# Layer 0 of a four-layer network: new slots for the steps of a hand-written schedule, and a new order of the steps within a slot

## The chip, the cores and the metric

The kernel runs on one core of one Trainium2 chip. The metric is the device time of one execution in microseconds (us); for a kernel it is given as the median of several executions. The core's engines run side by side, each in its own program order: TensorE (PE; its weight loads are PEld), VectorE (DVE), ScalarE (ACT), GpSimd (POOL) and SyncE (SP), whose queue issues nearly all DMAs. They wait for each other by semaphores.

## What is computed

Four layers follow each other on `x` of shape (4, 96, 64, 64): layer 0, which is changed, and three that stay as they are (a 7x7 depthwise convolution with a feed-forward part; attention without softmax and a quantized feed-forward part; a Fourier mixing step and another quantized feed-forward part). Layer 0 holds two Mamba blocks over each image's 4096 tokens, then a 1x1 convolution together with a pooled term, a normalization over the batch, and a residual. Cut to what matters:

```python
def _mamba_block(seq, ...):                      # seq: (4, 4096, 96), DIN = 192, DSTATE = 16
    h = layernorm(seq) * ln_g + ln_b
    xs, z = jnp.split(h @ in_w, 2, axis=-1)
    xc = silu(causal_conv4(xs) + conv_b)
    dbl = xc @ xproj_w
    dt, Bm, Cm = dbl[..., :6], dbl[..., 6:22], dbl[..., 22:]
    delta = softplus(dt @ dt_w + dt_b)
    dA = exp(delta[..., None] * A)               # per channel and state
    dBx = delta[..., None] * Bm[:, :, None, :] * xc[..., None]
    hstates = scan over tokens: hs[t] = dA[t] * hs[t - 1] + dBx[t]
    y = einsum('blds,bls->bld', hstates, Cm) + Dp * xc
    return (y * silu(z)) @ out_w                 # added to seq
```

192 channels times 16 states make 3072 recurrences per image and block, each over 4096 tokens. The scan is the bulk of the work.

## The kernel before

**Items and scans.** `layer0` (from line 147) works on 32 items: 4 stretches of 1024 tokens, times 2 blocks, times 4 images, in that order (the list `items`). An item has 24 scans, each one DVE instruction over 128 partitions (32 channels by 4 states) and 1024 tokens (L643). A scan is named (p, g, j): p is one of three parts of the channels, j one of two halves of a part, g one of four groups of states. `SLOTS['order']` gives the order: scans 0 to 5 are (0,0,0), (0,0,1), (0,2,0), (0,1,0), (0,1,1), (0,2,1); 6 and 7 are (0,3,0), (0,3,1); 8 to 17 are those of p = 1 and, mixed among the last of them, (2,3,0) and (2,3,1); 18 to 23 are the rest of p = 2.

**Slots.** The order of the instructions on PE, DVE, ACT and POOL is written out by hand: the loop at the end of `layer0` runs over steps m; `divmod(m, 24)` is the item k and the slot t. In slot t of item k DVE gets scan t of item k, and the other entries of `SLOTS` say in which slot each other step is put into its engine's order. A slot is only a place in the order; an engine starts an instruction when its turn comes and its semaphores are there. `SLOTS['seq']` gives the order of the kinds of steps within one slot. SP's DMAs are not held to the slots: they stand in SP's queue in about the order in which the steps were recorded, and each waits for its data and buffer, with all behind it.

**The steps of a slot.**
- `scan` (L623 on): for g = 0 and 1 a DVE product (L636) of `udb` (delta times xc, spread over the states) with `rep`, then the scan (L643). At j = 0 it takes one of four `hs` buffers from a first-in, first-out list.
- `fill` (L587 on): PE makes `rep` in one of two PSUM tiles. For g = 0 and 1 it spreads a row of B (L599). For g = 3, called GA, it transposes `uta` eight times (L594); `uta` is delta times xc times B, made by ACT in 32 weighings (L507), the entry `weigh`. `fills` gives how many slots ahead of its scan each fill stands.
- `exp` (L610): ACT makes `da`, the decay of a scan, three slots ahead (one slot ahead into PSUM, `dap`, for g = 2, called GP). `da` has three buffers.
- `b` (L621): GpSimd's product `up` for the scans of GP, at slots `b`. `c` (L648): GpSimd multiplies both halves of a finished (p, g) by C (`crep`), one slot behind its last scan; c(p, g) below.
- `start` (L658): PE begins y of a part with Dp times xc, at `starts`; `sum` (L665): PE adds a (p, g) after its c, at `sums` (a row for each p, an entry for each g), and this frees the `hs` buffer; `gate` (L677): DVE multiplies y by silu(z), at `gates` (values over 23 fall in the next item).
- `keep` (L654): ACT copies the last column of a finished scan into `state`.
- `end`: the output, at slots `ox` (load of x), `px` and `pz` (PE, L684 and L301), `fin` (ACT and the store, L710).
- `stages`: the first stage of the next item, function `first_stage` (L333 on). A slot value v of these entries stands at slot floor(v) - 24 counted from that item's scan 0, so 14.2 is slot 14 of the item before it and 28 is slot 4 of its own. Steps of one slot stand in the order of v. They are: load of x (`ln_ld`), the normalization (`ln_*`), the convolution's three products (`xc`, L287, with ACT's copies L411), Silu of xc and of the item before's z together with two loads of ACT's tables (`silu`, L422, L528, L304), `xproj` (PE, L301) and ACT's two copies into `dbl` (L441), delta's three products and copies, Softplus (`soft`, L449), the transposes of B (`tb`) and their copy (`bt`, L463), the stores `dd` and `du` (after GpSimd's product L479), z's products, `turn` and `keep` of delta times xc (L488, L493), the weighings, and the loads from DRAM `load_d` (`ddb`), `load_u` (`udb`), `load_c` (`crep`) and `load_b` (`brep`), four or eight DMAs of 128 KB each.

The loop itself:

```python
for m in range(first, last + 19):
    k, t = divmod(m, NTL)
    for step in SLOTS["seq"]:
        steps[step](m, k, t)
```

After the last item the totals of the batch normalization follow, and then layer 1.

Of the kernel before, what the change touches and what calls it, by code (L numbers as in the profile page):

```python
# [44 lines left out]
for _name, _w in [("A", 48), ("Dp", 6), ("c_b1", 3), ("f2_b1", 3), ("f3_b1", 3), ("id", 48), ("rd", 48), ("rb", 48), ("ib", 48)]:  # L45
# [2 lines left out]
NV128 = _n  # L48


SLOTS = {'ln_ld': -22,
 'ln_c': -9.4,
 'ln_sq': -9.2,
 'ln_sc': -7,
 'ln_t': -6.8,
 'ln_ev': -6.4,
 'xc': ((-6, -2.4), (-3.8, 0.4), (-1.2, 2.2)),
 'silu': 2.2,
 'xproj': 4.6,
 'dbl': 4.6,  # L60
 'delta': ((5.2, 6), (6, 7.4), (7.4, 8)),
 'soft': 8.2,
 'tb': 7.4,
 'dd': 8.6,
 'bt': 12.8,
 'du': 11.6,
 'z': ((11.4, 11.4), (10.8, 11.6), (12.6, 12.6)),
 'turn': (14.2, 15, 16),
 'keep': (14.4, 15.8, 16),
 'weigh': ((18, 5), (19, 4), (20, 6), (21, 2), (22, 2), (24, 7), (25, 1), (26, 2), (28, 3)),  # L70
 'load_d': ((14.4, 21.6), (24.6, 28.4), (29, 35.8)),
 'load_u': (14, 26.4, 33.6),
 'load_c': (20.2, 22.2, 24.8, 27.8),
 'load_b': 20.2,
 'fills': {(0, 1, 0): 2,
           (0, 3, 0): 1,
           (0, 3, 1): 1,
           (1, 0, 0): 1,
           (1, 3, 0): 1,
           (1, 1, 0): 1,  # L80
           (1, 3, 1): 1,
           (2, 3, 0): 1,
           (2, 3, 1): 1,
           (2, 0, 0): 1,
           (2, 1, 0): 2,
           (0, 0, 0): 1},
 'sums': ((7, 9, 8, 11), (13, 18, 17, 20), (24, 26, 26, 23)),
 'starts': (5, 13, 18),
 'gates': (13, 26, 31),
 'b': (2, 5, 8, 17, 20, 22),  # L90
 'fill0': -9,
 'ox': 25,
 'px': 33,
 'pz': 33,
 'fin': 34,
 'state': 1,
 'seq': ('scan', 'fill', 'end', 'start', 'b', 'keep', 'gate', 'c', 'sum', 'exp', 'stages'),
 'order': [(0, 0, 0), (0, 0, 1), (0, 2, 0), (0, 1, 0), (0, 1, 1), (0, 2, 1), (0, 3, 0), (0, 3, 1), (1, 0, 0),
           (1, 0, 1), (1, 2, 0), (1, 3, 0), (1, 1, 0), (1, 1, 1), (1, 2, 1), (2, 3, 0), (1, 3, 1), (2, 3, 1),
           (2, 0, 0), (2, 0, 1), (2, 2, 0), (2, 1, 0), (2, 1, 1), (2, 2, 1)]}  # L100
# [2 lines left out]
class Net:  # L103
# [43 lines left out]
    def layer0(self, dram, scratch):  # L147
        tc, nc, ins = self.tc, self.nc, self.ins
        x_in = ins["x"]
        with ExitStack() as ctx:  # L150
# [65 lines left out]
            def until(slot):  # L216
                for m in sorted(m for m in stages[0] if m <= slot - 24):
                    for _, f in sorted(stages[0].pop(m), key=lambda x: x[0]):
                        f()

            def prepare():
                with tc.tile_pool(name="l0s", bufs=1) as wk, tc.tile_pool(name="l0g", bufs=1) as sums_pool:
# [14 lines left out]
                    def spread_taps(q):  # L237
                        at = slice(q * MB, (q + 1) * MB)
                        ps = wide(C + 1, MB, q)
                        nc.tensor.matmul(ps, one, row[:, at], start=True, stop=True)  # L240
                        nc.vector.tensor_copy(taps[:, at], ps)
# [19 lines left out]

                    until(SLOTS["xc"][1][1])
                    spread_taps(2)
# [69 lines left out]
            def first_stage(k):  # L333
# [5 lines left out]
                def at_slot(t):  # L339
                    def keep(f):  # L340
                        steps.setdefault(int(t // 1) - 24, []).append((t, f))

                    return keep

                @at_slot(SLOTS["ln_ld"])
                def _():
                    m["xn"] = load_x(b, s, i) if k else x0


                @at_slot(SLOTS["ln_c"])  # L350
                def _():
# [9 lines left out]

                @at_slot(SLOTS["ln_sq"])
                def _():
# [15 lines left out]

                @at_slot(SLOTS["ln_sc"])  # L380
                def _():
# [3 lines left out]

                @at_slot(SLOTS["ln_t"])
                def _():
# [1344 lines left out]
```

## Time and profile before

| what | value |
|---|---|
| times of three runs | 3705.59, 3710.8, 3724.08 us; median 3710.8 |
| the profiled execution | 3723.78 us, of which the span of the profile is 3722.0 us |
| layer 0, first start to last end of a scan | 73.67 to 2449.02 us |
| mean ns of one scan, of one product on DVE | about 2340, about 1215 |
| mean ns of one product c, of one product `up` on POOL | 4187, 2363 |
| mean ns of one `da`, of one weighing on ACT | 1146, 441 |
| DMA, share of 16 engines over the span | 46.2% in queue q1 |

A page of the profile holds the busy time of each engine (part 1), the span in 40 equal slices of about 93 us, where each digit is the busy share of a slice in tenths (part 2), the DMA queues, the chain that ended last, and the costliest groups of instructions. Beside the page the trace answers questions: the waits, where a row such as `DVE hs L643 <- PE rep L594: 41.5, 34, 3.2` says that DVE, ahead of its instruction of line 643, was idle for 41.5 us in total, 34 times, 3.2 at most, until PE's instruction of line 594 released it; and the timeline, whose rows begin with the start and the busy time in us, then engine, line, operation and tiles, how many instructions stand in the row, and in brackets the idle time ahead of them with what ended it. Busy times of instructions that follow each other on one engine overlap by up to 0.1 us, so that steps are counted from start to start.

### The profile page before, as it was taken

To read this page: it belongs to the slowest core of one execution; us is meant where nothing else is said; L and a number is where in the kernel's file an instruction comes from. 1 tells how busy PE (TensorE), PEld (TensorE's weight loads), DVE (VectorE), ACT (ScalarE), POOL (GpSimd) and SP (SyncE) were. 2 spreads that over 40 slices of the span, in tenths; PEclk is the share of its full clock that TensorE was granted. 3 is DMA by queue.
4 is the path that set the end of the run, shared out by engine and by line. 5 is a ranking of instruction groups with operands and counts; after the bars stand their busy time and mean duration, and the time that the engine had idled before them with its cause. 6 is when DMAs were issued, how large, how long until landed. Compare 5 with 4: busy or idle time off the path is not lost. (4 is left out here: it accounts for less than half of the span.)

```text
span 3722.0 us, 47365 instructions
## 1 busy us (share of the span) xinstructions
PE 3098.0 (83%) x15360; PEld 1409.3 (38%) x15360; DVE 3020.9 (81%) x2966; ACT 2722.6 (73%) x5584; POOL 2567.9 (69%) x925
## 2 busy tenths in 40 slices
PE   7888788878887888888888878659798888999888
PEld 3332223222322232223222322228345436667643
DVE  5999999999999999999999999962665693444649
ACT  5888888887888887888888878641346786656557
POOL 1989988899899988998998999832001263444427
PEclk8999999989999999899999999859899998999989
DMA  7666656665666666666666666557000000011001
GB/s 186 151 162 155 170 152 161 156 169 153 160 155 169 160 153 156 172 158 152 158 171 160 148 165 160 145 149 272 12 0 1 1 1 6 24 35 47 24 12 58
DMA packets 171552, 446.36 MB, mean 120 GB/s; under 512 B 48756, under 2 KB 50750, under 8 KB 167968
## 3 DMA queue, kind: packets, MB, share of 16 engines
q1 hardware_dynamic: 171304, 443.34, 46.2%
q8 instruction: 121, 1.98, 0.2%
q14 instruction: 127, 1.04, 0.1%
HBM read 369.68 MB, written 73.50 MB: 119 GB/s over the span
## 5 line engine op out<-in xcount | busy, mean ns | idle before, releaser
L648 POOL TENSOR_TENSOR hs<-hs,crep 128x2048 f32<-128x2048 f32 x384 | 1601.7, 4187 | 224.4 <-DVE hs L643 177.2
L610 ACT ACTIVATE da<-ddb,nega 128x1024 f32<-128x1024 f32 x576 | 660.1, 1146 | 200.3 <-DMA ddb<-dd 129.1
L643 DVE TENSOR_TENSOR_SCAN hs<-da,state,rep 128x1024 f32<-128x1024 f32 x288 | 669.5, 2338 | 47.8 <-PE rep L594 28.0
L621 POOL TENSOR_TENSOR up<-udb,brep 128x1024 f32<-128x1024 f32 x192 | 453.6, 2363 | 83.3 <-DMA udb<-ud 62.2
L665 PE MATMUL y<-hs,sel_r 128*32 128x512 f32 x3072 | 462.2, 696 | 12.2 <-POOL hs L648 11.9
L599 PE MATMUL rep<-dbl,sel_b 32*128 32x512 f32 x768 | 249.9, 729 | 215.6 <-DVE hs L643 215.5
L507 ACT ACTIVATE uta<-delta,bt 128x192 f32<-128x192 f32 x1024 | 379.7, 441 | 0.0
L287 PE MATMUL ps<-n,w_x 97*64 97x512 f32 x1536 | 354.5, 604 | 12.5 <-ACT xc L411 11.8
L643 DVE TENSOR_TENSOR_SCAN hs<-da,state,u 128x1024 f32<-128x1024 f32 x144 | 338.1, 2348 | 23.7 <-PE y L665 7.8
L643 DVE TENSOR_TENSOR_SCAN hs<-dap,state,up 128x1024 f32<-128x1024 f32 x144 | 335.3, 2328 | 1.5 <-ACT dap L610 1.4
L594 PE MATMUL rep<-ident,uta 128*128 128x128 f32 x1536 | 223.0, 287 | 103.6 <-DVE hs L643 89.9
L594 PEld LDWEIGHTS rep<-ident,uta 128*128 128x128 f32 x1536 | 175.2, 146 | 248.6 <-issue 136.2
L636 DVE TENSOR_TENSOR u<-udb,rep 128x1024 f32<-128x1024 f32 x192 | 235.3, 1226 | 25.0 <-DMA udb<-ud 11.4
L643 DVE TENSOR_TENSOR_SCAN hs<-da,rep 128x1024 f32<-128x1024 f32 x96 | 218.0, 2281 | 19.5 <-PE rep L594 13.5
L610 ACT ACTIVATE dap<-ddb,nega 128x1024 f32<-128x1024 f32 x192 | 214.1, 1115 | 24.8 <-DVE hs L643 24.3
L636 DVE TENSOR_TENSOR rep<-udb,rep 128x1024 f32<-128x1024 f32 x192 | 231.8, 1207 | 0.0
L1290 POOL CAST hq<-y 128x1536 fp8e5<-128x1536 f16 x64 | 94.0, 1469 | 198.2 <-DVE y L1289 136.3
L287 PEld LDWEIGHTS ps<-n,w_x 97*64 97x64 f32 x1536 | 105.1, 137 | 259.1 <-issue 208.8
L665 PEld LDWEIGHTS y<-hs,sel_r 128*32 128x32 f32 x3072 | 73.9, 119 | 337.1 <-issue 261.7
L599 PEld LDWEIGHTS rep<-dbl,sel_b 32*128 32x128 f32 x768 | 65.8, 205 | 353.5 <-issue 299.1
L658 PE MATMUL y<-xc,dp 128*128 128x512 f32 x192 | 132.0, 778 | 31.3 <-ACT bt L463 31.3
L1157 POOL MEMSET h<- 1x4096 f32 x1 | 3.5, 3507 | 215.0 <-ACT g L1039 215.0
(287 smaller groups left out, 6291.6 us busy)
## 6 DMA issues: line engine op xcount, KB each, us to landing
udb<-ud SPq DMA_DIRECT2D x768, 128.0 KB
ddb<-dd SPq DMA_DIRECT2D x768, 128.0 KB
crep<-cd SPq DMA_DIRECT2D x512, 128.0 KB
dd<-delta SPq DMA_DIRECT2D x64, 384.0 KB
band<-in_band SPq DMA_DIRECT2D x24, 1024.0 KB
ud<-delta SPq DMA_DIRECT2D x62, 384.0 KB
brep<-cd SPq DMA_DIRECT2D x128, 128.0 KB
x<-in_x SPq DMA_DIRECT2D x32, 384.0 KB
```

The costliest lines, as they stand in the source:

```text
L287: nc.tensor.matmul(ps[rows], w[:, 64 * p : 64 * p + 64], rhs[:, at.start + shift : at.stop + shift], start=k == 0, stop=k == len(ws) - 1, ...
L507: nc.scalar.mul(m["uta"][:, q, :, 32 * s4 : 32 * s4 + 32].rearrange("t (p j) d -> t p j d", p=3), m["udt"][:, :, q].rearrange("t p (j d) - ...
L594: nc.tensor.transpose(x[:, q * 128 : q * 128 + 128], made[k]["uta"][:, q, 2 * h + j], self.ident)
L599: nc.tensor.matmul(x[:, at], sel_b[rows, g], made[k]["dbl"][rows, at], start=True, stop=True)
L610: nc.scalar.activation(da, made[k]["dd", h, j], AF.Exp, scale=nega[:, col : col + 1])
L621: nc.gpsimd.tensor_mul(up, made[k]["ud", p][:, j], made[k]["brep", GP])
L636: nc.vector.tensor_mul(u, made[k]["ud", h][:, j], x)
L643: nc.vector.tensor_tensor_scan(hs[:, 1:], made[k].pop(("da", t)), u, st, ALU.mult, ALU.add)
L648: nc.gpsimd.tensor_mul(hs[:, :, :T], hs[:, :, 1:], twice(made[k]["crep", g]))
L658: nc.tensor.matmul(y, dp[:, items[k][2], p], made[k]["xc"][:, p], start=True, stop=True)
L665: nc.tensor.matmul(made[k]["y", p][row : row + 32], sel_r, made[k]["hs", p, g][:, j, at], start=False, stop=True, skip_group_check=True,)
L1290: nc.gpsimd.tensor_copy(q, y2, saturate=False)
```

## The change

Only values in `SLOTS` change; no function does, and each instruction of layer 0 is still issued once for each item. The core of the diff:

```diff
-SLOTS = {'ln_ld': -22,
+SLOTS = {'ln_ld': -20.4,
...
- 'xc': ((-6, -2.4), (-3.8, 0.4), (-1.2, 2.2)),
- 'silu': 2.2,
+ 'xc': ((-6, -3.6), (-3.8, 0.4), (-1.2, 1.8)),
+ 'silu': 3.6,
...
- 'delta': ((5.2, 6), (6, 7.4), (7.4, 8)),
- 'soft': 8.2,
+ 'delta': ((5.2, 6.6), (6, 6.6), (7.2, 8.4)),
+ 'soft': 8.4,
...
- 'dd': 8.6,
+ 'dd': 9.2,
- 'du': 11.6,
- 'z': ((11.4, 11.4), (10.8, 11.6), (12.6, 12.6)),
- 'turn': (14.2, 15, 16),
- 'keep': (14.4, 15.8, 16),
- 'weigh': ((18, 5), (19, 4), (20, 6), (21, 2), (22, 2), (24, 7), (25, 1), (26, 2), (28, 3)),
- 'load_d': ((14.4, 21.6), (24.6, 28.4), (29, 35.8)),
- 'load_u': (14, 26.4, 33.6),
- 'load_c': (20.2, 22.2, 24.8, 27.8),
- 'load_b': 20.2,
- 'fills': {(0, 1, 0): 2,
+ 'du': 12.4,
+ 'z': ((12.4, 12.6), (12, 12.6), (13.6, 13.6)),
+ 'turn': (14, 15.4, 16.4),
+ 'keep': (14.4, 15.8, 16.8),
+ 'weigh': ((18, 2), (19, 2), (20, 11), (21, 6), (23, 3), (24, 1), (26, 1), (27, 1), (28, 5)),
+ 'load_d': ((18.4, 18.4), (25.6, 26.4), (29.2, 35.6)),
+ 'load_u': (13, 22.8, 33),
+ 'load_c': (21, 20.2, 24.4, 24),
+ 'load_b': 19.2,
+ 'fills': {(0, 1, 0): 1,
...
-           (1, 1, 0): 1,
+           (1, 1, 0): 2,
...
-           (2, 1, 0): 2,
+           (2, 1, 0): 1,
...
- 'sums': ((7, 9, 8, 11), (13, 18, 17, 20), (24, 26, 26, 23)),
+ 'sums': ((7, 9, 9, 11), (13, 16, 17, 18), (23, 27, 26, 22)),
  'starts': (5, 13, 18),
- 'gates': (13, 26, 31),
- 'b': (2, 5, 8, 17, 20, 22),
- 'fill0': -9,
- 'ox': 25,
+ 'gates': (13, 25, 29),
+ 'b': (0, 4, 13, 14, 19, 21),
+ 'fill0': -11,
+ 'ox': 32,
...
- 'seq': ('scan', 'fill', 'end', 'start', 'b', 'keep', 'gate', 'c', 'sum', 'exp', 'stages'),
+ 'seq': ('scan', 'exp', 'start', 'b', 'fill', 'gate', 'c', 'sum', 'end', 'keep', 'stages'),
```

The four values of `load_c` are for g = 3, 0, 1, 2; the six of `b` are for (0,1), (1,0), (1,1), (2,0), (2,1) and (0,0) of the next item.

In the order within a slot this moves `exp` ahead of the state copies, of the output's copies and of the stages on ACT; `start` ahead of `fill`, and the output's products behind the sums, on PE. On DVE and POOL the order of the kinds within a slot stays.

## The prediction

> **What bounds the kernel now.** I read the page first: parts 1 and 2 say which engine is full, and when.
>
> ```profile
> PE 3098.0 (83%) x15360; PEld 1409.3 (38%) x15360; DVE 3020.9 (81%) x2966; ACT 2722.6 (73%) x5584; POOL 2567.9 (69%) x925
> ...
> DVE  5999999999999999999999999962665693444649
> ```
>
> The whole change lies in layer 0, and DVE is at 9 in every slice of layer 0 but the first. Its scans run from 73.67 us (first start) to 2449.02 us (last end): 32 items, mean 74.3 us from scan 0 to the next scan 0 (shortest 72.1, longest 77.4). So only DVE's idle time can be won, and the second view is what DVE waits for in that stretch:
>
> ```profile
> DVE hs L643 <- PE rep L594: 41.5, 34, 3.2
> DVE hs L643 <- PE y L665: 9.9, 32, 0.7
> ```
>
> The first row is nearly all one place: scan 7 of an item, (0,3,1), waits for fill(7), TensorE's eight transposes of `uta`. From the timeline, scan 6 to scan 7 takes 3.69 us on average over items 3 to 29 where other scans follow each other in 2.25: 1.44 us per item. Third view, the timeline of item 18 (scan 0 at 1409.88), where it is worst:
>
> ```profile
> 1427.09 1.13 ACT L507 ACTIVATE uta<-delta,bt 128x192 f32<-128x192 f32 x3
> 1428.13 1.04 ACT L441 COPY dbl<-ps 102x512 f32<-102x512 f32 x2
> ...
> 1428.54 1.92 PE L658 MATMUL y<-xc,dp 128*128 128x512 f32 x2
> ...
> 1430.38 1.98 PE L287 MATMUL ps<-dbl,dtw 103*64 103x512 f32 x4
> ...
> 1432.29 1.97 PE L594 MATMUL rep<-ident,uta 128*128 128x128 f32 x8
> ...
> 1434.37 2.35 DVE L643 TENSOR_TENSOR_SCAN hs<-da,state,rep 128x1024 f32<-128x1024 f32 x1 [3.23 <-PE rep L594]
> ```
>
> Behind fill(6) TensorE's queue holds the start of y (L658), then delta's first product (L287), which needs ACT's `dbl` copies, and only then fill(7). The same four steps in item 21 (TensorE alone):
>
> ```profile
> 1650.72 1.32 PE L594 MATMUL rep<-ident,uta 128*128 128x128 f32 x8 [1.73 <-DVE hs L643]
> 1651.88 1.02 PE L658 MATMUL y<-xc,dp 128*128 128x512 f32 x2
> 1652.83 1.08 PE L287 MATMUL ps<-dbl,dtw 103*64 103x512 f32 x4
> 1653.84 1.09 PE L594 MATMUL rep<-ident,uta 128*128 128x128 f32 x8
> ```
>
> Here each is half as long, and scan 7 hardly waits (0.06 us). Items fall into these two kinds: the start takes 1.5 to 1.9 us in 19 of items 1 to 30, about 1.02 in 11. ACT's own largest wait is the fourth view (300 to 2400 us):
>
> ```profile
> ACT da L610 <- DMA ddb<-dd: 117.1, 29, 5.5
> ```
>
> That is 4 us per item, before exp(1): its rows `ddb`(0,1) are issued on SP behind a `crep` load that waits for GpSimd. DVE has cover there, but ACT comes late to the next slots.
>
> **The change, part by part.** Times count from scan 0 of an item; "e5" is the end of scan 5.
>
> *Order within a slot, start and fill.* TensorE gets start(0) of slot 5 ahead of fill(6) instead of behind it. There it lies in TensorE's wait for e4 (idle 2.01 us in item 18, 1.73 in 21), so it costs nothing; if `xproj` ended over 1 us later it would delay fill(6). What fill(7) then waits for is the end of the `dbl` copies, plus 0.1, plus delta's product, plus its own time. Doing this for items 1 to 30 with each item's own durations, fill(7) ends **0.59 us** earlier on average (0.06 in items of the short kind, about 1.0 in the long).
>
> *ACT: exp leads, silu from 2.2 to 3.6, `weigh`, `load_d`.* `load_d`(0,1) goes from 21.6 to 18.4, ahead of the `brep` and `crep` loads: the 4 us wait goes. 24 instead of 19 of the 32 weighings come before slot 24: five at 0.345 = 1.7 us more there. ACT is so 2.3 us early at slot 0 and next waits for e0 (dap(2)'s bank) and e1 (the state copy of slot 2), e1 = 5.92. From there, with start-to-start times of item 17: state copy 0.10, weighing 0.35, exp(6) 1.05, weighing 0.35 (silu begins at about 7.8); table, silu, silu of z, table 5.45; dap(5) 1.04; exp(7) 1.04; five weighings 1.73; `dbl` 1.05: end at 18.1. Before it is 18.29 in item 17 and 18.35 on average. **0.25 us** earlier.
>
> *gate(2) from slot 7 to 5, gate(1) from 2 to 1.* DVE's work stays. gate(2) (0.6 us) leaves the stretch from scan 7 to 11, and this gives nothing: from the end of fill(7) to that of fill(11) TensorE runs without a break for 12.33 us (items 10, 12, 17, 20, 25), and scan 11 starts 0.05 us behind fill(11) in most of them. DVE would need 11.7 for its part now, so it waits the 0.6 at scan 11 instead. What counts is when fill(7) ends, both terms above.
>
> *GpSimd's products.* up(1,1) goes from slot 8 to 13, up(2,0) from 17 to 14: both now between du and c(1,1), where GpSimd idles 4.3 us, for 4.7 us. Worked through with item-by-item times, c(1,3) ends 1.9 us after scan 18 starts. The sum (1,3) moves to slot 18, ahead of xc's first product; TensorE reaches it 1.46 us after scan 18 now, so 0.4 us of waiting. fill(21) then ends at 7.6; DVE wants it at 8.2. Hidden by 0.65, and fill(0) of the next item by 0.5 (0.94 now less 0.4). The other sums, `up` slots, and fill leads have over 0.8 us each between ready and needed; an `hs` slot is free at least as early as now, so the 9.9 us of the second row may shrink: I take nothing.
>
> *SP's queue.* ddb(1,0) and (1,1) now stand behind `crep`2, which waits for c(2,2) (ends at 7.6 in item 18). Eight `crep` issues and four `ddb` at about 0.45: 13.3; landing about 3.5 later (item 18's ddb(0,1): last issue ends at 71.6, exp(1) starts at 75.1): 16.8. ACT comes to exp(8) at 18.1: hidden by 1.3. `x` for the output (`ox` 25 to 32) follows `cd`, at about 20.5; x0 took 4.6 us from issue to its first reader (1.7 to 6.3), TensorE wants it at 27: hidden by 2.
>
> *Ends.* At the start ACT does an `xc` copy (0.47 us) ahead of exp(0): +0.5. At the end the last two sums of y both wait for c(2,2) where now one is done before; one took 1.93 us there: **+2**, once.
>
> *Sum.* 31 x (0.59 + 0.25) = 26, less 2.5: 23.5 us. The profiled execution took 3723.8 us (span 3722.0), 13 above the median of 3710.8. 3700.3/3723.8 of the median is **3687**. Bounds: the first term from 0.06 to 1.0, the second from 0 (weighings eat ACT's lead) to 0.5: 31 x 0.06 - 2.5 = nothing, to 31 x 1.5 - 2.5 = 44.
>
> **The rivals.**
>
> 1. *TensorE stays in its short kind.* The start now fills part of the gap ahead of fill(6). If this makes all items like item 21 there, fill(7) ends 1.12 us earlier instead of 0.59: 31 x 1.37 - 2.5 = 40, **3671**. For: the rows of items 18 and 21, a factor of two. Against: the gaps change by under 1 us, and the 6.5 us gap before fill(3) stays. [...]
>
> 2. *The gain is met by a next wait.* fill(11), fill(21) and fill(0) all have under 1 us of cover, dap(23) about 0.4. If 0.5 of the 0.84 us comes back there: 31 x 0.34 - 2.5 = 8, **3703**. For: the shortest interval now, 72.1, shows how little is left. Against: these covers are worked out, and each wait shifts the next.
>
> 3. *Slower: TensorE queues behind GpSimd at sum (1,3).* If c(1,3) ends more than 0.65 us later than worked out (`brep` late, products slower than 2.36), xc's products, fill(21) and scan 21 move 1:1. At 2.5 us late: 31 x (2.5 - 0.65) = 57 against 26: **3744**. For: du, two products and three c's now run without a gap. Against: GpSimd catches up before c(1,0) in every item from 2 to 29 (c(1,0) starts 0.15 to 0.45 us after e9).
>
> That the change does nothing is no rival: the built order has start ahead of fill(6), and the loads moved, in every item.
>
> **How the numbers follow.** Forecast (3677 to 3698) 0.42; TensorE short (3655 to 3677) 0.20; met by a next wait (3698 to 3724) 0.27; slower (above 3724) 0.11. Likeliest: 3687. The range 3655 to 3724 leaves out the slower case. About 0.5% (18.6 us) is what a measurement of this kernel tells from no change. Faster by more than that is below 3692: all of the second case and four fifths of the first, 0.54. Slower by more is above 3729: 0.10. Within: 0.36.
>
> **What would show it.** In the profile after: L658 of slot 5 ahead of fill(6); `dbl` copies ending near 18.1; the wait of scan 7 on L594 down from 1.44 to about 0.4, with some 0.6 to 0.9 at scan 11; ACT's wait for `ddb` near nothing; c(1,3) ending about 2 us after scan 18 starts. A wait of scan 21 on L599 or of L665 on GpSimd in slot 18 speaks for the third rival; ACT waiting for `ddb` at exp(8), or L684 for `x`, would make the queue's covers wrong.

## The result, and the profile after

The changed kernel takes 3674.31 us (median of four runs, 3669.73 to 3680.34) against 3717.44 us for the kernel before beside it (four runs, 3705.59 to 3726.27): ratio **0.9886** [0.9862, 0.9909], 1.1% faster. The forecast was 3687, the range 3655 to 3724. The profiled execution of after took 3669.73 us (span 3667.9), 54 us less than the profiled one of before (span 3722.0), where the medians differ by 43. Of the 54 us, 47.4 are won by the end of the last scan (the scans run from 70.26 to 2401.61 us, before from 73.67 to 2449.02). The other 6.7 lie behind it, where layers 1 to 3 did not change: from the last scan to the end the profiled executions of this study take 1262.9 to 1278.3 us.

Parts 1 and 2 of the page of after, the lines that answer to those shown of before:

```profile
PE 3058.8 (83%) x15360; PEld 1409.8 (38%) x15360; DVE 3021.3 (82%) x2966; ACT 2730.2 (74%) x5584; POOL 2567.7 (70%) x925
...
DVE  5999999999999999999999999952665683444649
```

DVE's work is the same (3021 us); it is only packed closer. TensorE's busy time is 39 us shorter for the same 15360 matmuls: a first sign that matmuls ran faster, not only sooner.

DVE's waits in layer 0 of after (columns: us in total, times, longest):

```profile
DVE hs L643 <- PE rep L594: 6.5, 5, 3.6
DVE hs L643 <- ACT dap L610: 3.1, 5, 1.3
DVE hs L643 <- PE y L665: 1.7, 2, 1.1
```

The first row was 41.5 us and the third 9.9. Most of what is left falls in item 0: from 150 us to the last scan no row of DVE is above 0.9 us. DVE hardly waits now, and the period (scan 0 to scan 0, mean of items 1 to 30, as all periods below) went from 74.22 to 72.62 us.

The timeline of after, item 18 again (scan 0 at 1380.8):

```profile
1394.55 1.12 PE L658 MATMUL y<-xc,dp 128*128 128x512 f32 x2
...
1397.08 1.37 PE L594 MATMUL rep<-ident,uta 128*128 128x128 f32 x8 [1.40 <-DVE hs L643]
1397.97 1.04 ACT L441 COPY dbl<-ps 102x512 f32<-102x512 f32 x2
1398.59 1.55 PE L287 MATMUL ps<-dbl,dtw 103*64 103x512 f32 x4
...
1399.67 4.58 DVE L643 TENSOR_TENSOR_SCAN hs<-da,state,rep 128x1024 f32<-128x1024 f32 x2
...
1400.07 1.09 PE L594 MATMUL rep<-ident,uta 128*128 128x128 f32 x8
```

The start (L658) stands ahead of fill(6) and takes 1.12 us, not 1.92. Delta's product (L287) begins after the first of the two `dbl` copies; its 1.55 us hold the wait for the second. fill(7) takes 1.09 us, not 1.97, and is done at 1401.16, 0.8 us before scan 7 (the second of the two scans in the row) wants it: DVE no longer waits. Before, TensorE was idle twice around fill(6) of this item, the second time for a weighing (L507) that ACT made late:

```profile
1426.17 0.96 PE L594 MATMUL rep<-ident,uta 128*128 128x128 f32 x7 [2.01 <-DVE hs L643]
1428.28 0.47 PE L594 MATMUL rep<-ident,uta 128*128 128x128 f32 x1 [1.15 <-ACT uta L507]
```

The clock granted to TensorE can be read for a stretch. For before: from the last transpose of fill(6) of item 18 on, then from the start of fill(6) of item 21 on (the number that stands ahead of the last two of a row is the clock; 1.00 is full):

```profile
1428.30:1434.20 5.90, 5.90 (x17) 2.46 (x17) 2.61 (x2) 3.83 (x7) 5.90 (x2) 0.50 0.64 160
1650.70:1654.90 4.20, 4.14 (x24) 2.19 (x24) 4.20 (x2) 3.14 (x8) 4.11 (x1) 1.00 0.58 139
```

The "long kind" is half clock (0.50 against 1.00 in these rows). By the clock records, items 1 to 30 of before have 19 half-clock stretches that begin 14 to 22 us after scan 0; after has none. Both kernels keep one at the beginning of each of these items (1.6 to 5.1 us after scan 0 in before, 0.5 to 3.7 in after), while TensorE idles for 6.0 to 7.4 us ahead of fill(3).

ACT's waits in after, 300 to 2400 us:

```profile
ACT dap L610 <- DVE hs L643: 120.5, 62, 7.1
...
ACT delta L493 <- DMA ddb<-dd: 7.2, 17, 0.5
```

The 117.1 us row for `ddb` ahead of exp is gone; ACT waits for DVE now.

### The profile page after: what moved, and what is told of

Read it like the earlier page. It is cut to its first block, busy times and chain, and to the rows that moved or that the text cites. A ratio compares the mean times of both kernels' runs of the same rounds, so it can differ in the third digit from the quotient of the medians.

```text
span 3667.9 us, 47180 instructions
## 1 busy us (share of the span) xinstructions
PE 3058.8 (83%) x15360; PEld 1409.8 (38%) x15360; DVE 3021.3 (82%) x2966; ACT 2730.2 (74%) x5584; POOL 2567.7 (70%) x925
## 3 DMA queue, kind: packets, MB, share of 16 engines
q14 instruction: 124, 1.02, 0.1%
## 5 line engine op out<-in xcount | busy, mean ns | idle before, releaser
L665 PE MATMUL y<-hs,sel_r 128*32 128x512 f32 x3072 | 453.8, 684 | 32.8 <-POOL hs L648 32.0
L507 ACT ACTIVATE uta<-delta,bt 128x192 f32<-128x192 f32 x1024 | 381.8, 442 | 0.0
L287 PE MATMUL ps<-n,w_x 97*64 97x512 f32 x1536 | 352.5, 601 | 0.5 <-DVE w_x L252 0.5
L287 PEld LDWEIGHTS ps<-n,w_x 97*64 97x64 f32 x1536 | 104.6, 137 | 241.9 <-issue 199.5
L1429 POOL TENSOR_TENSOR av<-av,ec 128x780 f32<-128x780 f32 x32 | 58.8, 1836 | 133.0 <-ACT av L1426 133.0
```

Of the source, the lines that this page charges most:

```text
L287: nc.tensor.matmul(ps[rows], w[:, 64 * p : 64 * p + 64], rhs[:, at.start + shift : at.stop + shift], start=k == 0, stop=k == len(ws) - 1, ...
L507: nc.scalar.mul(m["uta"][:, q, :, 32 * s4 : 32 * s4 + 32].rearrange("t (p j) d -> t p j d", p=3), m["udt"][:, :, q].rearrange("t p (j d) - ...
L665: nc.tensor.matmul(made[k]["y", p][row : row + 32], sel_r, made[k]["hs", p, g][:, j, at], start=False, stop=True, skip_group_check=True,)
L1429: nc.gpsimd.tensor_add(v[:, 2:4], v[:, 0:2], ec)
```

## The experiments

The theory after the result: the gain is that TensorE is not throttled (put to half clock) around fill(6), because the idle time there got shorter. The rival: the start's place in the chain gives the gain, by the order alone. In what follows **S** is the start ahead of fill in the order of the steps, **L** the four load slots, **R** all the rest of the change. "Half clock" counts the items of 30 with slow products behind fill(6); "idle" is TensorE's mean idle time from the end of `xproj` to the end of fill(6). Each ratio is against runs of the kernel before on the same chip.

**S alone** (in before):

```diff
- 'seq': ('scan', 'fill', 'end', 'start', 'b', 'keep', 'gate', 'c', 'sum', 'exp', 'stages'),
+ 'seq': ('scan', 'start', 'fill', 'end', 'b', 'keep', 'gate', 'c', 'sum', 'exp', 'stages'),
```

> The kernel before with one edit: start moved ahead of fill in the order within a slot. Before, the start of y (L658) takes 1.52 us on average between fill(6) and delta's first product. Theory (order and speed: the start leaves the chain to fill(7), and in the idle gap ahead of fill(6) it also keeps TensorE at its short durations): start about 1.1 us in all items, fill(7) ends 2.15 us behind the dbl copies as in the changed kernel, near 20.7 instead of 21.9, an item takes about 73.0 us instead of 74.2, ratio 0.988 to 0.992. Rival 1 (order alone, TensorE as slow as before in two items of three): fill(7) 0.6 us earlier, ratio 0.995. Rival 2 (ACT's late dbl copies are the bound, so that the loads matter more): dbl copies end later against scan 0, ratio 0.997 to 1.000.

Measured: 0.9925 [0.9899, 0.9951], period 73.17. No start is slow, and fill(7) ends at 20.64 us after scan 0 instead of 21.90. This is the theory's answer, with the ratio just above its band. One swap gives nearly two thirds of the gain in period.

**The start twice, early and late** (in before). The extra pair of products is added work, done with the same data:

```diff
+            def starting_early(k, at):
+                if at == starts[0]:
+                    start_y(k, 0)
...
+            steps |= {"early": of_y(starts, starting_early)}
...
- 'seq': ('scan', 'fill', 'end', 'start', 'b', 'keep', 'gate', 'c', 'sum', 'exp', 'stages'),
+ 'seq': ('scan', 'early', 'fill', 'end', 'start', 'b', 'keep', 'gate', 'c', 'sum', 'exp', 'stages'),
```

> The kernel before, where TensorE does the start of y of slot 5 twice: once ahead of fill(6), into the idle gap, and once more at its old place behind it (the same product into the same bank, so that the result stays). The chain to fill(7) keeps the start; only the gap is filled. Theory that the gap sets TensorE's speed: the second start, delta's product and fill(7) take their short times (about 1.0, 1.1, 1.1 us) in nearly all items, the wait of scan 7 falls from 1.44 to about 0.4 us, ratio about 0.991. Rival (speed has nothing to do with this gap): durations as before, two items of three slow, ratio 1.000.

Measured: 0.9915 [0.9891, 0.9939], period 73.08: as good as S alone, although the start is back in the chain. Item 18 of it:

```profile
1403.74 1.13 PE L658 MATMUL y<-xc,dp 128*128 128x512 f32 x2
1404.78 1.43 PE L594 MATMUL rep<-ident,uta 128*128 128x128 f32 x8
1406.05 1.02 PE L658 MATMUL y<-xc,dp 128*128 128x512 f32 x2
1407.00 1.08 PE L287 MATMUL ps<-dbl,dtw 103*64 103x512 f32 x4
1408.01 1.09 PE L594 MATMUL rep<-ident,uta 128*128 128x128 f32 x8
```

The gap ahead of fill(6) is filled, all behind it is short, and the second L658 costs 1 us where the one in before cost up to 1.92. This speaks against the rival: with the start in the chain again fill(7) ends only 0.11 us later than with S alone (20.75).

**The start back** (in after):

```diff
- 'seq': ('scan', 'exp', 'start', 'b', 'fill', 'gate', 'c', 'sum', 'end', 'keep', 'stages'),
+ 'seq': ('scan', 'exp', 'b', 'fill', 'start', 'gate', 'c', 'sum', 'end', 'keep', 'stages'),
```

> The changed kernel with start behind fill again, all else kept. Theory (order and speed): the gap ahead of fill(6) is back at about 2 us and the start is in the chain; with slow durations fill(7) ends near 21.5 instead of 20.3 and fill(11) near 33.8, where scan 11 wants it by 32.9: 0.9 us per item in the slow ones, ratio against before 0.993 to 0.997. Rival (TensorE stays fast because the rest of the new order keeps it busy): fill(7) near 20.6, ratio 0.989, as the changed kernel.

Measured: 0.9944 [0.9924, 0.9964], period 73.30, the ratio in the theory's band; half clock is back in 13 items. About half of the gain goes with S.

**The start a slot earlier** (in after):

```diff
- 'starts': (5, 13, 18),
+ 'starts': (4, 13, 18),
```

> The changed kernel with the first start in slot 4 instead of 5: it then stands ahead of xproj, so neither in the chain to fill(7) nor in the gap ahead of fill(6). Theory that the filled gap keeps TensorE fast: some items slow, delta's product and fill(7) near 1.9 us there, fill(11) late by 0.3 to 0.6 us, ratio 0.990 to 0.993. Rival (only the place in the order counts): as the changed kernel, 0.9886, all durations short.

Measured: 0.9891 [0.9869, 0.9913], period 72.61, as after: a miss for the theory as I had put it, and the time that I had given the rival. What failed is the premise that the gap comes back. In slot 4 the start pushes `xproj` back, so the idle time around fill(6) stays (0.83 us, in after 0.82), and fill(7) ends at 20.26 all the same. The start itself, which now runs closer behind the 7 us of idle ahead of fill(3), takes 1.25 to 1.80 us in 16 items instead of 1.12, and this costs nothing. Since the idle time did not change, this run does not decide between the two.

**The start twice, in after** (`early` is the step of the other kernel with two starts):

```diff
- 'seq': ('scan', 'exp', 'start', 'b', 'fill', 'gate', 'c', 'sum', 'end', 'keep', 'stages'),
+ 'seq': ('scan', 'exp', 'early', 'b', 'fill', 'start', 'gate', 'c', 'sum', 'end', 'keep', 'stages'),
```

> The changed kernel with the start of y in slot 5 done twice: once ahead of fill(6) and, with the same products, once more behind it, so that delta's product and fill(7) stand behind a start again, as in the variant with the start moved back (ratio 0.9944, period 73.30 us). The two products are work added. Theory (what the early start brings is a shorter gap, and with it TensorE's short kind): every start, delta product and fill(7) short (about 1.05 to 1.1 us), fill(7) ends at about 20.7 us after scan 0, still ahead of where DVE wants it (21.05), period 72.6 to 72.8, ratio 0.988 to 0.990. Rival (the place in the chain counts): fill(7) at 21.1, scan 7 waits, period about 73.3, ratio 0.993 to 0.995.

Measured: 0.9885 [0.9864, 0.9906], period 72.69, no half clock behind fill(6), fill(7) at 20.47. Item 19 with the start back, then with the start twice, TensorE alone:

```profile
1480.81 1.39 PE L594 MATMUL rep<-ident,uta 128*128 128x128 f32 x8 [2.28 <-DVE hs L643]
1482.01 1.90 PE L658 MATMUL y<-xc,dp 128*128 128x512 f32 x2
1483.84 1.85 PE L287 MATMUL ps<-dbl,dtw 103*64 103x512 f32 x4
1485.62 1.09 PE L594 MATMUL rep<-ident,uta 128*128 128x128 f32 x8
...
1469.60 1.12 PE L658 MATMUL y<-xc,dp 128*128 128x512 f32 x2
1471.98 1.37 PE L594 MATMUL rep<-ident,uta 128*128 128x128 f32 x8 [1.25 <-DVE hs L643]
1473.19 1.02 PE L658 MATMUL y<-xc,dp 128*128 128x512 f32 x2
1474.14 1.08 PE L287 MATMUL ps<-dbl,dtw 103*64 103x512 f32 x4
1475.15 1.09 PE L594 MATMUL rep<-ident,uta 128*128 128x128 f32 x8
```

Against the start back (0.9944) the only difference is two more products, and they make it faster. The theory holds.

**The gates of before** (in after):

```diff
- 'gates': (13, 25, 29),
+ 'gates': (13, 26, 31),
```

> The changed kernel with the gates at slots (13, 26, 31) again. The prediction said that the move of gate(2) from slot 7 to slot 5 gives nothing. Theory now: DVE's work per item is the same and fill(7) ends at 20.3, so scan 7 at 21.05 less 0.6 for the missing gate still finds it ready by 0.2; scan 11 finds fill(11) (32.55) ready either way: period 72.6 to 72.7, ratio 0.988 to 0.990. Rival (the early gate is what lets fill(7) be in time): 0.6 us of each item comes back as a wait at scan 7: period about 73.2, ratio about 0.994.

Measured: 0.9869 [0.9847, 0.9891], period 72.44. The early gates give nothing; the old ones are, if anything, 0.18 us per item better.

**The loads of before** (in after):

```diff
- 'load_d': ((18.4, 18.4), (25.6, 26.4), (29.2, 35.6)),
- 'load_u': (13, 22.8, 33),
- 'load_c': (21, 20.2, 24.4, 24),
- 'load_b': 19.2,
+ 'load_d': ((14.4, 21.6), (24.6, 28.4), (29, 35.8)),
+ 'load_u': (14, 26.4, 33.6),
+ 'load_c': (20.2, 22.2, 24.8, 27.8),
+ 'load_b': 20.2,
```

> The changed kernel with the load slots of before (load_d, load_u, load_c, load_b). Theory: ACT waits some 4 us for ddb ahead of exp(1) again, catches up part of it by its slack at dap(2), and ends the dbl copies 0.3 to 0.9 us later; fill(7), now at 20.3, has 0.8 us to spare ahead of scan 7, so little of this reaches DVE: period 72.6 to 73.0, ratio 0.989 to 0.992. Rival (the loads are the second main part of the gain, beside the start): all that the changed kernel has over the one with the start alone moved (period 73.17, ratio 0.9925) goes: period 73.2 or more, ratio 0.993 or more.

Measured: 0.9881 [0.9857, 0.9905], period 72.65: nothing lost. The period is in the theory's band, the ratio just under it; but ACT's wait did not come back as I had expected (ACT's waits, 300 to 2400 us of this kernel):

```profile
ACT da L610 <- issue: 61.8, 29, 3.7
...
ACT da L610 <- DMA ddb<-dd: 23.4, 23, 2.5
```

It is 0.8 us per item, not 4. So R ends most of this wait by itself. R alone, run below under "S and L back", shows the same (300 to 2400 us of that kernel, against 117.1 us in before):

```profile
ACT da L610 <- DMA ddb<-dd: 18.3, 19, 2.2
```

A likely reason, not shown: with GpSimd's products in new slots the last-but-one c of an item ends 0.9 us after the next scan 0, in before 2.6, so the queue ahead of `ddb` may be released earlier.

**L alone** (in before; the four entries of the last diff the other way round):

```diff
- 'load_d': ((14.4, 21.6), (24.6, 28.4), (29, 35.8)),
+ 'load_d': ((18.4, 18.4), (25.6, 26.4), (29.2, 35.6)),
...
```

> The kernel before with the load slots of after alone. Theory: ACT's wait for ddb ahead of exp(1) (4 us per item) goes, but the start still stands behind fill(6) and the gap ahead of it stays about 2 us, so TensorE's long kind stays in over half of the items: dbl ends 0 to 0.5 us earlier, ratio 0.996 to 1.001. Rival (with ACT early all of the chain is early): scan 7 loses most of its 1.4 us wait, ratio below 0.993.

Measured: 0.9935 [0.9915, 0.9955], period 73.11: a miss, much more than I gave it. ACT ends the `dbl` copies 0.8 us earlier (at 17.70), and the wait of fill(6) for a weighing is gone, so the idle time falls from 2.32 to 1.85 us and half clock from 19 items to 9. In before fill(7) ends at 22.64 in the 19 slow items and at 20.61 in the others, so ten slow items fewer are worth some 0.7 of the 1.15 us by which fill(7) comes earlier; the rest is that the chain starts earlier. Items 24 and 25 of it, TensorE alone:

```profile
1843.36 1.06 PE L594 MATMUL rep<-ident,uta 128*128 128x128 f32 x8 [2.15 <-DVE hs L643]
1844.26 1.45 PE L658 MATMUL y<-xc,dp 128*128 128x512 f32 x2
1845.64 1.98 PE L287 MATMUL ps<-dbl,dtw 103*64 103x512 f32 x4
1847.55 1.36 PE L594 MATMUL rep<-ident,uta 128*128 128x128 f32 x8
...
1917.59 1.06 PE L594 MATMUL rep<-ident,uta 128*128 128x128 f32 x8 [1.73 <-DVE hs L643]
1918.49 1.02 PE L658 MATMUL y<-xc,dp 128*128 128x512 f32 x2
1919.45 1.08 PE L287 MATMUL ps<-dbl,dtw 103*64 103x512 f32 x4
1920.46 1.09 PE L594 MATMUL rep<-ident,uta 128*128 128x128 f32 x8
```

With 2.15 us idle ahead of fill(6) the products behind it are slow, with 1.73 they are not. In this kernel 2.04 us is the longest idle time of an item with short products, and 2.07 the shortest of one with long ones. The border is not as sharp elsewhere: in before items with up to 2.39 us stay short and others are long from 2.09 on, and with S alone two items are long at 1.63.

**S and L** (in before):

```diff
- 'seq': ('scan', 'fill', 'end', 'start', 'b', 'keep', 'gate', 'c', 'sum', 'exp', 'stages'),
+ 'seq': ('scan', 'start', 'fill', 'end', 'b', 'keep', 'gate', 'c', 'sum', 'exp', 'stages'),
...
- 'load_d': ((14.4, 21.6), (24.6, 28.4), (29, 35.8)),
+ 'load_d': ((18.4, 18.4), (25.6, 26.4), (29.2, 35.6)),
...
```

> The kernel before with two parts of the change alone: start ahead of fill in the order within a slot (alone: ratio 0.9925, period 73.17) and the load slots of after (alone: 0.9935, 73.11). Theory (both shorten the same chain fill(6), start, delta product, fill(7), and DVE's own work is the floor): together they end the wait of scan 7 in all items, period 72.4 to 72.8, ratio 0.986 to 0.990, not the 0.986 of the two added only if the floor were lower. Rival (the floor of after needs the other edits too, those on ACT, GpSimd and the sums): period 73.0 to 73.2, ratio 0.992 or above.

Measured: 0.9871 [0.9858, 0.9885], period 72.58: the whole gain, without R. Scan 7's wait is gone, and GA's transposes hardly hold DVE at all (DVE's waits in this kernel):

```profile
DVE hs L643 <- PE y L665: 10.5, 34, 0.6
DVE hs L643 <- PE rep L594: 1.3, 2, 0.8
```

The 0.3 us per item for y ahead of a gate, the first row, is still there and costs nothing in the sum: the old gates stand ahead of a product, where a gate adds 0.4 to 0.5 us to the interval (4.19 and 4.30 us with it in before, 3.76 and 3.79 at the same two places without it in after), and the new ones ahead of a scan, where it adds 0.6 (2.84 us with a gate, 2.25 without, medians of after).

**S and L back, R alone** (in after):

```diff
- 'seq': ('scan', 'exp', 'start', 'b', 'fill', 'gate', 'c', 'sum', 'end', 'keep', 'stages'),
+ 'seq': ('scan', 'exp', 'b', 'fill', 'start', 'gate', 'c', 'sum', 'end', 'keep', 'stages'),
...
- 'load_d': ((18.4, 18.4), (25.6, 26.4), (29.2, 35.6)),
+ 'load_d': ((14.4, 21.6), (24.6, 28.4), (29, 35.8)),
...
```

> The changed kernel with both of these parts taken back: the start behind fill and the load slots of before. Left are the moves of ACT's weighings and silu, GpSimd's products, sums, gates and the output. Theory (they give little by themselves): TensorE's long kind in over a third of the items, scan 7 waits again, period 73.3 to 74.0, ratio 0.994 to 0.999. Rival (the changed kernel does not need the loads, with or without the early start): as with the start alone taken back, period 73.3, ratio 0.9944.

Measured: 0.9929 [0.9917, 0.9942], period 73.17, half clock in 10 items. A miss: R gives by itself as much as S or L. In it too ACT is earlier (`dbl` ends at 18.12, in before at 18.50). Which of R's edits does this was not tried.

**After with the old gates and a better end, beside after once more:**

```diff
- 'sums': ((7, 9, 9, 11), (13, 16, 17, 18), (23, 27, 26, 22)),
+ 'sums': ((7, 9, 9, 11), (13, 16, 17, 18), (23, 26, 27, 22)),
...
- 'gates': (13, 25, 29),
+ 'gates': (13, 26, 31),
```

> The changed kernel with the gates of before, (13, 26, 31), which alone gave period 72.44, and the sums (2,0) and (2,1) at 26 and 27 in place of 27 and 26 of the entries for g = 1 and 2, so that one of the last two sums is done before the last product c is. Theory: 0.18 us in each of 31 items and up to 2 us at the end, 6 to 8 us less than the changed kernel beside it (0.2%). Rival: within 2 us of it (0.05%), the difference of the single runs having been chance.

> The changed kernel once more, so that the variant with the gates of before is compared with it on one chip. All theories: ratio 0.987 to 0.990, period 72.6.

Measured: 0.9869 [0.9855, 0.9882] with the edits, 0.9870 [0.9855, 0.9885] for after again; medians 3669.24 and 3671.29 us. The periods are 72.48 and 72.62, so the profiles still show 0.14 us per item, but the times don't tell the two apart: the rival's answer. No version clearly beats after, where DVE has hardly a wait left.

S, L and R in all eight combinations (fill(7) ends so many us after scan 0):

| parts | ratio | period | fill(7) | idle | half clock |
|---|---|---|---|---|---|
| none (before) | 1 | 74.22 | 21.90 | 2.32 | 19 |
| S | 0.9925 | 73.17 | 20.64 | 0.96 | 2 |
| L | 0.9935 | 73.11 | 20.75 | 1.85 | 9 |
| R | 0.9929 | 73.17 | 21.00 | 1.92 | 10 |
| L, R | 0.9944 | 73.30 | 21.15 | 2.03 | 13 |
| S, R | 0.9881 | 72.65 | 20.26 | 0.83 | 0 |
| S, L | 0.9871 | 72.58 | 19.97 | 0.69 | 0 |
| S, L, R (after) | 0.9886 | 72.62 | 20.26 | 0.82 | 0 |

Each part alone takes 1.05 to 1.11 us from the period; two of them, if one is S, take 1.57 to 1.64, and the third adds nothing. L and R both make ACT earlier and end most of fill(6)'s wait for a weighing, and they do not add to each other.

## Why the prediction was right in sign and range, and too small

The sum forecast 24 us less, and 43 were measured. Per item 1.61 us were won, where the sum had 0.84, between bounds of 0.06 and 1.5.

- **The start, 0.59 us: the step that failed.** "Doing this for items 1 to 30 with each item's own durations" took the durations as given. They changed: behind fill(6) the 19 items that ran at half clock went to full clock. S alone ended fill(7) 1.26 us earlier, all parts 1.64. The place in the chain, which the step priced, is worth 0.1 to 0.2 us once the products are short (start twice against S alone, and against after); most of the rest is the durations. This is the first rival (TensorE in its short kind, 3671 us, chance 0.20), and 3674.31 lies in its band. I had held against it that "the gaps change by under 1 us"; the idle time around fill(6) fell from 2.32 to 0.82.
- **ACT, 0.25 us.** `dbl` ends at 18.11 as worked out (18.1), 0.39 before the mean of before, which is 18.50 over items 1 to 30 and not the 18.35 of the working. But an earlier ACT brings more than this: it ends TensorE's wait for the weighing inside fill(6), which I left out, and with it half of the throttled items (with L alone 9, in before 19). L alone is worth 1.11 us per item. `ddb`'s wait is gone, as forecast. (Of the new order on ACT, exp only passes the state copies and the output's copies: ahead of the stages it stood in before, too.)
- **gate(2) gives nothing: right, for another reason.** TensorE still takes 12.29 us from fill(7) to fill(11) (worked out: 12.33), but fill(7) is so early that fill(11) ends at 32.55, ahead of scan 11 at 32.90. The 0.6 to 0.9 us that I forecast at scan 11 are not there (scan 10 to 11: 2.25 us), and scan 7 has 0.8 us to spare instead of 0.4 to wait. DVE has no wait there that the move could fill.
- **GpSimd and the sum (1,3): right.** c(1,3) ends 1.97 us after scan 18 starts (forecast 1.9); the sum waits 0.53 us in the median (forecast 0.4), and fill(21), which ends 7.8 us after scan 18 (forecast 7.6) where DVE wants it at 8.2, hides it. The third rival's mechanism is there but never reaches scan 21.
- **SP's queue: right.** Neither `ddb` at exp(8) nor `x` holds anyone (one wait of 2.7 us for `ddb` from 300 to 2350 us).
- **The ends: right, at the start by luck.** Scan 0 of item 1 comes 0.4 us later (forecast 0.5), but not for one copy ahead of exp(0): the first scan starts 3.4 us earlier, and item 0 takes 3.8 us more. The last sum of y ends 9.9 us after the last scan instead of 8.2 (+1.7, forecast 2).
- **The second rival** (the gain met by a next wait) is out: DVE's waits in layer 0 sum to 3.6 us from 150 to 2390 us.

In sum: 30 items by 1.61 are 48.3 us, less 0.4 at the start and 0.4 in the last item: 47.4 to the end of the scans, where 26 less 0.5 were forecast. Of the 1.61, scan 7's wait is 1.46 (3.70 to 2.24 from scan 6). The rest is many small amounts, at most 0.08 us in any other interval of two scans, less 0.12 that the earlier gates add; I had taken both at nothing.

## What to carry to other kernels

A duration from a trace need not be a constant of the instruction: in before the start took 1.02 us in some items and up to 1.92 in others. Where the same matmul shows two durations a factor of two apart, ask what decides between them before multiplying: here an edit that cut TensorE's idle time (S alone, 2.32 to 0.96 us) took half clock behind fill(6) from 19 items to 2, and so changed the durations of what stands there. Filling this gap of TensorE with work that has to be done anyway paid here, even with work done twice (0.9915 in before; 0.9885 in after, against 0.9944 without the second start). And parts that each shorten the same wait didn't add up: alone they took 1.05 to 1.11 us from the period, all three together 1.61. Once DVE, which bounds layer 0, hardly waited, the next edit gave nothing, so measure the parts alone and together.

## What the runs showed of the hardware

The clock records of the traces change only between 1.0 and 0.5, at times on a grid of 3413.33 ns: all 189 changes of before lie within 2 ns of it, over the whole execution, and so do the 109 of after. Cutting items 1 to 30 of before along this grid, 546 windows begin at full clock, and 66 of them are followed by half clock. A split at 1.85 us of TensorE's busy time in the window says whether the next window is at half clock in all but 10 of the 546; in after, a split at 1.7 to 1.8 sorts all 549, of which 30 are followed by half clock. Each of the 65 changes back to full clock in this stretch of before came after a window that was busy for 3.1 us or more, though some windows as busy were followed by half clock still. The profile models the ends of matmuls, so these busy times are approximate.

Around fill(6) the idle time alone does not tell the two kinds of items apart: in before it was 2.09 to 3.16 us in the 19 items with half clock and 1.06 to 2.39 in the other 11, in after at most 1.56, with half clock in none. Of the windows at full clock that this stretch (end of `xproj` to end of fill(6)) touches, the least busy one does so in before: TensorE was busy in it for 0.84 to 1.50 us in the 19 items, for 1.57 to 2.53 in the 11. That the busy time within a window decides is my reading of these counts; no experiment separates it from the idle time.
